# Turning x1 into tokens: TensorE transposes replaced by VectorE block transposes and on-chip DMAs

## The chip, the cores and the metric

The kernel runs on one core of a Trainium2 chip. The metric is device time in microseconds (us), the median of several runs. The page and the trace come from one further, profiled execution.

## The reference

Everything is float32, for 32 images of 128 channels x 64 x 64 pixels. The third line of the first block is a 3x3 convolution done in a learned "butterfly" transform domain.

```python
# layer 0
x = x + conv(group_norm(x))          # _gn, then _kop2d with the butterfly matrices
# layer 1, on tokens: t[b] is 4096 tokens x 128 channels
t = x.reshape(B, C, H * W).transpose(0, 2, 1)
t = t + attention(layer_norm(t))     # 128x128 probabilities per image, from the sum over tokens of k v^T
t = t + experts(layer_norm(t))       # 8 experts, the best 2 of each token, weighed by a softmax
x = t.transpose(0, 2, 1).reshape(B, C, H, W)
```

x1 below is x after layer 0, which lies with channels on partitions. Layer 1 needs it with tokens on partitions, 32 tiles of 128 tokens per image.

## The kernel before

The program has three stages in time. Stage one normalises each image, transforms it forward and puts it into DRAM (xf). Stage two multiplies in the transform domain, one of 64 columns after another, and puts the products into DRAM (pf). Stage three, which the change touches, takes the images one after another as a software pipeline: it loads r from pf, transforms back along w (`w_inverse`, copied into u by `w_out` on ScalarE), then along h (`h_inverse`), adds the image (`h_out`, on VectorE, which writes x1 into `ys[b]`), turns x1 into tokens, and runs attention and experts on them.

Every piece of work in stage three is an entry of a plan: a key, an engine, an estimated duration, what it comes after, and what room it takes (PSUM tiles "pe" and "tl", rings for r, and so on). The order in which pieces are issued is written out by hand in `ORDER`: a list of `key:stage` words for one period. Image b's piece stands at b + stage + (place in the list), shifted for the first two and the last two images by the numbers in `EDGE`. Each engine works strictly in that order, and so does SP, whose queue issues the DMAs. The keys used below:

- `r0` to `r7`, `x` (SP): loads of the transformed products and of the image.
- `w`, `wo`, `h`, `ho`: inverse along w, its copy by ScalarE, inverse along h, its sum by VectorE.
- `pt` (TensorE) and `to` (ScalarE), eight of each per image: `turn` transposes four 128x128 tiles of x1 into a PSUM tile (L1066), `turned` copies it into the token buffer `tk[b % 2]` (L1071). `pt` waits for `so` of the image two before, which last reads that buffer.
- `sa` (VectorE): the statistics of the tokens (L1035, L1037). `pwa`, `na` (ScalarE, GpSimd): their reciprocal root.
- `xg` (ScalarE, L1101) and `pg` (TensorE, L1112): the normalised tokens and their Gram matrix. `gs` to `prx`: the small chain of the attention's softmax.
- `pp`, `at`, `ad`: the attention's product, its scaling, its sum into the tokens (L1185, L1196, L1211), with the statistics for the second norm.
- `pwb` to `gt`: the router. `xn`, `px`, `xT`: normalised tokens, turned for the experts.
- `pe` (TensorE, L1323): the experts, two PSUM tiles of 128x512 per 128 tokens. `m` (VectorE, L1334) weighs them by the gates, `s` (GpSimd, L1359 to L1362) sums them into the tokens.
- `so` (VectorE, L1368): block transposes of the finished tokens. A VectorE transpose turns each block of 32x32 within its 32 partitions; the store `os` (SP, L1378) puts the blocks into their places in DRAM.
- `prep`: once, corrections of the weights for the norms' means.

The experts' PSUM tiles come from a pool of three (`eps`), the "tl" tiles from a pool of two.

Of the kernel before, what the change touches and what calls it, by code (L numbers as in the profile page):

```python
# [10 lines left out]
F32 = mybir.dt.float32  # L11
# [92 lines left out]
def kernel(  # L104
# [732 lines left out]
    kvb = kc.tile([P, 2, P], F32, name="kvb")  # L837
    nc.gpsimd.dma_start(kvb[:, 0, :], bk.partition_broadcast(P))
    nc.gpsimd.dma_start(kvb[:, 1, :], bv.partition_broadcast(P))
    u = up.tile([P, n, P], F32, name="u")  # L840
    tk = [ct.tile([P, NT, P], F32, name=f"tk{i}") for i in range(2)]
    xg = [ct.tile([P, 4, P], F32, name=f"xg{i}") for i in range(NG)]
# [26 lines left out]
    plan = Plan({"cv": 1, "pe": 3, "tl": 2, "r": 8, "xg": NG, "xn": 2, "tm": 2, "so": 2})  # L869
# [34 lines left out]
    def conv(b):  # L904
# [12 lines left out]
        def w_out(e, oh):  # L917
            def run():
                ps = tile_of["cv", b, e]
                for r in range(2):  # L920
                    nc.scalar.copy(  # L921
                        u[r * n : (r + 1) * n, :, oh * n + 8 * e : oh * n + 8 * e + 8],
                        ps[oh * n : (oh + 1) * n, :, r * n : (r + 1) * n].rearrange("h o w -> h w o"),
                    )
            return run
# [88 lines left out]
        for e in range(8):  # L1014
            at = b + 0.08 * e
            add(b, f"w{e}", "PE", 1.9, at, w_inverse(e), [f"r{e}"] + [(b - 1, f"h{k}") for k in range(4)], ("cv",), ("r",))
            for oh in range(2):
                add(
                    b, f"wo{e}_{oh}", "ACT", 1.2, at, w_out(e, oh),
                    [f"w{e}"] + [(b - 1, f"h{k}") for k in range(4)], (), ("cv",) if oh else (),  # L1020
                )
# [5 lines left out]
    def front(b):  # L1027

        t = tk[b % 2]
        v = {}  # L1030

        def bn(which, lo, hi):
            bs = st.tile([P, 4, 6], F32, name=f"bs{which}_{b}_{lo}", tag="bs", bufs=2)
            for i in range(lo, hi):
                nc.vector.bn_stats(bs[:, i - lo, :], t[:, i, :])  # L1035
# [24 lines left out]
        def turn(g):  # L1060
            def run():
                ps = tile_of["pt", b, g] = tps.tile([P, 512], F32, tag="tl", name=f"pt{b}_{g}")
# [6 lines left out]
        def turned(g):  # L1069
            def run():  # L1070
                nc.scalar.copy(  # L1071
                    t[:, 4 * g : 4 * g + 4, :].rearrange("p k c -> p (k c)"), tile_of.pop(("pt", b, g))
                )
            return run
# [10 lines left out]
        for g in range(8):  # L1085
            at = s1 + 0.016 * g
            add(b, f"pt{g}", "PE", 0.48, at, turn(g), [(b - 2, f"so{g}")] + [f"ho{k}" for k in range(4)], ("tl",))
            add(b, f"to{g}", "ACT", 0.55, at, turned(g), [f"pt{g}"], (), ("tl",))
            add(b, f"sa{g}", "DVE", 0.85, at, stats1(g), [f"to{g}"] + (["sa0"] if g else []))
        if b == 0:  # L1090
            add(b, "prep", "PE", 3.5, 1.2, prepare, [f"sa{g}" for g in range(8)], ("pe",), ("pe",))
        add(b, "pwa", "ACT", 3.1, s1 + 0.14, lambda: power(1), [f"sa{g}" for g in range(8)])
        add(b, "na", "POOL", 1.7, s1 + 0.14, lambda: newton(1), ["pwa"])


        def norm(g):
            def run():
                rstd, nmr, above = (v[1][:, k, :] for k in range(3))
                for k in range(4):
                    i = 4 * g + k  # L1100
                    nc.scalar.activation(  # L1101
                        xg[g % NG][:, k, :], t[:, i, :], AF.Identity, bias=above[:, i : i + 1], scale=rstd[:, i : i + 1]
# [3 lines left out]
        def gram(g):  # L1106
            def run():
                if g == 0:
                    v["pg"] = tps.tile([P, 512], F32, tag="tl", name=f"pg{b}")
                for k in range(4):  # L1110
                    i = 4 * g + k
                    nc.tensor.matmul(  # L1112
                        v["pg"][:, 0:P], xg[g % NG][:, k, :], xg[g % NG][:, k, :],
# [4 lines left out]
        for g in range(8):  # L1118
            at = s1 + 0.26 + 0.016 * g
            add(b, f"xg{g}", "ACT", 1.65, at, norm(g), ["na", (b if g >= NG else b - 1, f"pg{(g - NG) % 8}")], ("xg",))  # L1120
# [85 lines left out]
        def added(lo, m):  # L1206
            def run():
# [3 lines left out]
                nc.vector.tensor_tensor(t[:, lo : lo + m, :], ps[:, :, 0:P], t[:, lo : lo + m, :], ALU.add)  # L1211
# [79 lines left out]
    def experts(b):  # L1291
        t = tk[b % 2]

        def normal(g):
            def run():
                rstd, nmr = tile_of["norm", b]
                x = tile_of["xn", b, g] = wp.tile([P, 4, P], F32, tag="xn", name=f"xn{b}_{g}")
                for k in range(4):
                    i = 4 * g + k
                    nc.scalar.activation(  # L1300
                        x[:, k, :], t[:, i, :], AF.Identity, bias=nmr[:, i : i + 1], scale=rstd[:, i : i + 1]
# [39 lines left out]
        def weighed(i, half):  # L1341

            def run():
                ps = tile_of.pop(("pe", b, i, half))
                for e in range(4):
                    nc.vector.scalar_tensor_tensor(  # L1346
                        t[:, i, :], ps[:, e * P : (e + 1) * P], tile_of["gate", b][:, i, 4 * half + e : 4 * half + e + 1],
                        t[:, i, :], ALU.mult, ALU.add,
# [6 lines left out]
        def summed(j):  # L1355
            def run():
# [4 lines left out]
                for m in range(2):  # L1361
                    nc.gpsimd.tensor_tensor(t[:, lo : lo + 2, :], t[:, lo : lo + 2, :], tm[:, :, m, :], ALU.add)  # L1362
            return run

        def flip(g):
            def run():
# [3 lines left out]
                    in_=t[:, 4 * g : 4 * g + 4, :].rearrange("p t (k c) -> p t k c", c=32),  # L1370
# [44 lines left out]
    for b in range(B):  # L1415
# [5 lines left out]
        s1:4 px2:4 m4_0:4 pe5_0:4 xT2:4 m5_1:4 pwa:3 pe6_0:4 ho0:2 px3:4 pe4_1:4 h1:2 m4_1:4 xn6:4 m5_0:4 na:3  # L1421
        m6_0:4 pe6_1:4 ho1:2 s2:4 xg0:3 pe7_1:4 pe7_0:4 m7_0:4 m6_1:4 h2:2 xT3:4 so0:4 xg2:3 xg1:3 m7_1:4 pe8_0:4
        ho2:2 pe9_0:4 s3:4 m8_0:4 xg3:3 pe8_1:4 m9_0:4 pg0:3 m8_1:4 pg1:3 pe9_1:4 xg5:3 pe10_1:4 pe10_0:4 m9_1:4
        xg4:3 pe11_0:4 s4:4 m10_0:4 pg2:3 so1:4 pg3:3 xg6:3 os1:4 xg7:3 pg4:3 pe11_1:4 xn5:4 pg5:3 m11_1:4 m11_0:4
        pg6:3 r1:1 m10_1:4 pg7:3 s5:4 pe12_0:4 gs:3 pe13_1:4 m12_0:4 pb:3 pe12_1:4 t1:3 pe13_0:4 os0:4 r2:0 pb2:3
        h3:2 sm:3 m13_0:4 pr:3 xT4:4 sr:3 m12_1:4 sn:3 m13_1:4 pe14_0:4 s6:4 m14_0:4 pc:3 pe15_1:4 pe15_0:4 prx:3
        ho3:2 pp0:3 m15_0:4 px5:4 at0:3 pe14_1:4 m15_1:4 pe19_0:4 m14_1:4 xT5:4 ad0:3 pe18_0:4 xn7:4 s7:4 pp6:3
        m18_0:4 pe19_1:4 at6:3 pp9:3 w0:1 m19_0:4 m19_1:4 at9:3 ad6:3 pe18_1:4 r7:1 wo0_0:1 ad9:3 pe16_0:4 wo0_1:1
        pp21:3 m18_1:4 pe16_1:4 at21:3 m16_0:4 so3:4 s9:4 pp12:3 m16_1:4 w1:1 at12:3 ad21:3 r4:0 x:1 os3:4 pe17_1:4
        wo1_0:1 ad12:3 pe17_0:4 wo1_1:1 pp24:3 m17_1:4 pe22_0:4 m17_0:4 at24:3 s8:4 pp3:3 m22_0:4 w2:1 at3:3 ad24:3  # L1430
        pe23_0:4 ad3:3 wo2_0:1 pe22_1:4 wo2_1:1 pp30:3 m22_1:4 pe23_1:4 m23_0:4 at30:3 pp15:3 m23_1:4 w3:1 ad30:3
        at15:3 s11:4 so4:4 pe21_1:4 ad15:3 wo3_0:1 r5:0 os4:4 px6:4 pe20_0:4 wo3_1:1 pe20_1:4 m20_0:4 xT6:4 pp18:3
        m20_1:4 pe21_0:4 m21_1:4 at18:3 pp27:3 m21_0:4 w4:1 at27:3 s10:4 ad18:3 pe26_0:4 ad27:3 wo4_0:1 pe27_1:4
        pe26_1:4 m26_0:4 pwb:3 m27_1:4 pt0:2 so2:4 pe24_0:4 m26_1:4 pe27_0:4 m24_0:4 pt1:2 m27_0:4 to0:2 nb:3
        pe25_1:4 to1:2 so5:4 wo4_1:1 pe25_0:4 m25_1:4 os5:4 s13:4 px7:4 m25_0:4 pe24_1:4 xT7:4 l2:3 xn0:3 pt2:2 f1:3
        w5:1 f2:3 pt5:2 pe30_0:4 m24_1:4 wo5_0:1 f3:3 pe31_0:4 wo5_1:1 s12:4 pe30_1:4 m30_0:4 to2:2 to5:2 w6:1 sa0:2
        m31_0:4 m30_1:4 pe31_1:4 pt4:2 m31_1:4 pt3:2 to4:2 f4:3 pe28_1:4 px0:3 pe29_1:4 sa5:2 wo6_0:1 s15:4 sa4:2
        wo6_1:1 sa1:2 pe28_0:4 w7:1 xn1:3 f5:3 xT0:3 to3:2 m28_0:4 so6:4 m28_1:4 m29_1:4 os6:4 pe29_0:4 xn4:3 pt6:2
        m29_0:4 px1:3 gt:3 pe0_0:3 s14:4 to6:2 pe1_1:3 m0_0:3 r6:0 os2:4 pe0_1:3 m1_1:3 wo7_0:1 pe1_0:3 pe3_0:3
        px4:3 wo7_1:1 sa6:2 m1_0:3 m0_1:3 pe2_0:3 xn3:3 xn2:3 xT1:3 sa2:2 s0:3 pe3_1:3 m2_0:3 h0:1 m3_1:3 so7:4  # L1440
        m3_0:3 sa3:2 os7:4 pe2_1:3 pt7:2 r0:0 r3:0 pe4_0:3 pe5_1:3 m2_1:3 to7:2 sa7:2
# [3 lines left out]
            at:-0.001152 f:0.024239 gs:-0.002876 gt:0.000645 h:-0.088197 ho:-0.107173 l:-0.011950 m:-0.001978  # L1445
            na:-0.062269 nb:0.023962 os:0.037831 pb:-0.003357 pc:0.004368 pe:-0.004859 pg:-0.007392
            prep:-0.061921 prx:-0.000723 pt:-0.339605 pwa:-0.154931 pwb:0.037324 px:0.004889 r:-0.551854
            s:-0.000175 sa:-0.148905 sm:-0.006267 sn:0.000807 so:-0.001240 sr:0.003296 t:-0.002368 to:-0.321139
            w:-0.120521 wo:-0.109642 x:0.001867 xT:0.001275 xg:0.001692 xn:0.024691
        """,  # L1450
        1: """
            ad:0.003202 at:0.005763 f:0.005458 gs:-0.006322 gt:-0.000499 h:0.054990 ho:0.051746 l:-0.039944
            m:-0.001956 na:-0.011054 nb:-0.006237 os:0.010755 pc:-0.007414 pe:-0.000758 pg:0.001613 pr:-0.004399
            prx:-0.010090 pt:-0.015523 pwa:0.002034 pwb:0.001095 px:-0.002083 r:0.003449 s:-0.001956 sa:0.014227
            sn:-0.012403 so:-0.008148 sr:-0.010178 t:0.008140 to:0.002048 w:-0.000799 wo:-0.000193 xT:-0.009151
            xg:0.001343 xn:0.009969
        """,
        B - 2: """
            ad:-0.000137 at:0.005214 f:0.009800 gt:0.013838 h:-0.001798 ho:-0.002170 l:0.001614 m:0.011670
            na:0.002329 nb:-0.000549 os:0.199427 pb:-0.000148 pc:-0.004225 pe:0.008786 pg:-0.022172 pp:-0.005288  # L1460
            pr:-0.000058 prx:-0.004077 pt:-0.004342 pwa:-0.000635 pwb:-0.005281 px:0.016961 r:-0.007120
            s:0.049524 sa:-0.000213 sm:0.000159 sn:0.010880 so:0.176068 sr:0.012703 t:0.003951 w:0.001356
            wo:-0.009915 x:0.098978 xT:0.012789 xg:0.005833 xn:0.039799
        """,
        B - 1: """
            ad:0.016785 at:0.025250 f:0.011554 gt:0.005035 h:0.014633 ho:-0.003864 m:0.001746 na:0.022282
# [76 lines left out]
```

## Time and profile before

| | us |
|---|---|
| median of 3 runs (5923.06 to 5928.99) | 5924.06 |
| the profiled execution | 5924.1 |
| its span, first to last instruction | 5922.4 |
| stage three begins, about | 2542 |
| an image in the steady part of stage three | 101.8 |

On the page, busy time is the union of an engine's instructions; DMA-issuing instructions, which are all that SP runs, are not counted. "PE" is TensorE's matmuls, "PEld" its weight loads, "DVE" VectorE, "ACT" ScalarE, "POOL" GpSimd, "SPq" SP's queue. A row of the windows gives, for a stretch of time, its length, the busy time of each engine with its number of instructions, the granted TensorE clock, and the share and rate of DMA. A row of groups gives line, engine, operation, output and inputs, shape, count, then busy time and mean duration in ns, then the idle time ahead of it. A row of the timeline gives start, duration and what ran.

### The profile page before, as it was taken

The page shows a single profiled execution, that of the slowest core. Times are in us where ns is not written, and L with a number is a line of the kernel's source. Part 1 is how long each engine was busy: PE and PEld are TensorE (multiplying, and loading weights), DVE is VectorE, ACT ScalarE, POOL GpSimd, SP SyncE. Part 2 cuts the span into 40 slices and gives each one's busy share as a digit, 9 for nine tenths or more (in the row PEclk, how much of TensorE's full clock was granted, in tenths as well). Part 3 has the DMA queues.
Part 4 walks back from the last instruction along what each step waited for, and adds up shares of the span by engine and source line. Part 5 has one row for each costly group of instructions (what it writes and reads, how often), then busy time and mean ns, then how long its engine had stood idle before and what let it go on. Part 6 is the DMA issues. An engine that isn't in the chain of part 4 may idle for free. (4 is left out here: it accounts for less than half of the span.)

```text
span 5922.4 us, 221064 instructions
## 1 busy us (share of the span) xinstructions
PE 5789.1 (98%) x94348; PEld 4560.4 (77%) x94348; DVE 4235.4 (72%) x10353; ACT 3837.7 (65%) x7089; POOL 3947.6 (67%) x4210
## 2 busy tenths in 40 slices
PE   7999999999999999979999999999999999999997
PEld 7999999999999999976666666666666666666653
DVE  5565555555555555538888878788888888787877
ACT  7666664555555555557777777777777777777762
POOL 2110006666666666607888888888888888888887
PEclk9999999999999999989999999999999999999999
DMA  5767766666666666652323222233223222222201
GB/s 194 241 228 233 236 210 206 171 174 171 171 173 173 172 172 173 158 159 61 97 76 87 79 79 87 82 88 83 88 75 97 76 84 81 79 86 83 77 21 29
DMA packets 664681, 756.88 MB, mean 128 GB/s; under 512 B 70608, under 2 KB 462288, under 8 KB 659600
## 3 DMA queue, kind: packets, MB, share of 16 engines
q1 hardware_dynamic: 661088, 733.69, 43.0%
q8 instruction: 740, 12.12, 0.9%
q0 software_dynamic: 2608, 9.06, 0.5%
q14 instruction: 245, 2.01, 0.1%
HBM read 406.79 MB, written 335.54 MB: 125 GB/s over the span
## 5 line engine op out<-in xcount | busy, mean ns | idle before, releaser
L1323 PE MATMUL pe<-ew_sb,xT 128*128 128x512 f32 x4096 | 1973.2, 600 | 36.6 <-DVE tm L1334 22.8
L1334 DVE TENSOR_TENSOR tm<-pe,oh 128x512 f32<-128x512 f32 x2028 | 1298.4, 678 | 369.1 <-PE pe L1323 259.4
L1359 POOL TENSOR_TENSOR tm<-tm 128x512 f32<-128x512 f32 x1014 | 1270.4, 1272 | 287.0 <-DVE tm L1334 282.2
L1323 PEld LDWEIGHTS pe<-ew_sb,xT 128*128 128x128 f32 x4096 | 691.8, 190 | 552.1 <-issue 325.3
L660 DVE COPY f<-g 128x1024 f32<-128x1024 f32 x508 | 622.4, 1225 | 651.9 <-PE g L649 651.9
L671 PE MATMUL m<-f,s 128*64 128x64 f32 x32768 | 1071.3, 224 | 1.7 <-ACT f L660 0.8
L671 PEld LDWEIGHTS m<-f,s 128*64 128x64 f32 x32768 | 1001.1, 138 | 63.2 <-issue 2.5
L617 POOL COPY s<-l 128x512 f32<-128x512 f32 x512 | 546.2, 1102 | 527.3 <-issue 510.4
L660 ACT COPY f<-g 128x1024 f32<-128x1024 f32 x508 | 514.9, 1014 | 562.4 <-PE g L649 536.3
L1362 POOL TENSOR_TENSOR tk<-tk,tm 128x256 f32<-128x256 f32 x1014 | 737.9, 728 | 79.5
L1360 POOL TENSOR_TENSOR tm<-tm 128x512 f32<-128x512 f32 x507 | 644.7, 1272 | 39.8
L649 PE MATMUL g<-c,wst 9*128 9x128 f32 x16256 | 601.2, 284 | 4.5 <-issue 4.1
L921 ACT COPY u<-pu 64x512 f32<-64x512 f32 x960 | 558.0, 581 | 67.8 <-PE pu L910 58.7
L1196 ACT ACTIVATE pp<-pp,ln 128x128 f32<-128x128 f32 x1024 | 442.3, 432 | 230.9 <-PE pp L1185 157.2
L649 PEld LDWEIGHTS g<-c,wst 9*128 9x128 f32 x16256 | 504.0, 187 | 39.5 <-issue 4.8
L619 POOL TENSOR_SCALAR s<-l 128x512 f32<-128x512 f32 x256 | 509.6, 1991 | 0.0
L362 POOL TENSOR_TENSOR grstd<-gms,mhalf 128x1 f32<-128x1 f32 x32 | 17.7, 554 | 736.4 <-DVE gms L358 736.4
L431 PE MATMUL pf<-ph,v 128*128 128x128 f32 x4096 | 491.2, 278 | 5.5 <-ACT z L396 1.1
L910 PEld LDWEIGHTS pu<-qw,r 128*128 128x128 f32 x3840 | 456.8, 193 | 34.0 <-ACT u L921 22.2
L431 PEld LDWEIGHTS pf<-ph,v 128*128 128x128 f32 x4096 | 466.9, 192 | 15.5 <-ACT z L396 7.2
L910 PE MATMUL pu<-qw,r 128*128 128x128 f32 x3840 | 471.2, 276 | 4.9 <-ACT u L921 4.8
L1035 DVE BATCH_NORM_STATS2 bs<-tk 128x6 f32<-128x128 f32 x2048 | 449.5, 280 | 24.5 <-ACT tk L1071 23.2
(176 smaller groups left out, 7978.4 us busy)
## 6 DMA issues: line engine op xcount, KB each, us to landing
xf<-f SPq DMA_DIRECT2D x512, 256.0 KB
pf<-o SPq DMA_DIRECT2D x1016, 128.0 KB
l<-xf SPq DMA_DIRECT2D x1012, 128.0 KB
r<-pf SPq DMA_DIRECT2D x496, 256.0 KB
x<-in_x_dram SPq DMA_DIRECT2D x256, 256.0 KB
out_dram<-so SPq DMA_DIRECT2D x1024, 64.0 KB
y<-in_x_dram SPq DMA_DIRECT2D x31, 2048.0 KB
r<-pf POOLq DMA_DIRECT2D x16, 248.0 KB, 8.3
```

The source lines that it names most:

```text
L431: nc.tensor.matmul(pl[:, j * P : (j + 1) * P], vs[b][:, 8 * g + j, :], ph.rearrange("h r m -> h (r m)"), start=True, stop=True,)
L617: nc.gpsimd.tensor_copy(dst, src)
L649: nc.tensor.matmul(pg[g // 2][:, g % 2, m * P : (m + 1) * P], wst[rows, 16 * half + 4 * t + m, :], c[rows].rearrange("r h k -> r (h k)"), ...
L660: copy(f.rearrange("i m (g o) -> i m g o", g=2), tile_of["g", w, half, t][k].rearrange("i g (o m) -> i m g o", o=4))
L671: nc.tensor.matmul(ps[hh * n : (hh + 1) * n, q, :], s[:, h].rearrange("i k b -> i (k b)")[:, B * r : B * r + n], f[:, h, r, :], start=(r = ...
L910: nc.tensor.matmul(ps[:, k, :], rs[b, e][:, k * P : (k + 1) * P], qw.rearrange("w r m -> w (r m)"), start=True, stop=True,)
L921: nc.scalar.copy(u[r * n : (r + 1) * n, :, oh * n + 8 * e : oh * n + 8 * e + 8], ps[oh * n : (oh + 1) * n, :, r * n : (r + 1) * n].rearran ...
L1323: nc.tensor.matmul(ps, tile_of["xT", b, i // 4][:, i % 4, :], ew_sb[:, es, :].rearrange("d e c -> d (e c)"), start=True, stop=True,)
L1334: nc.vector.tensor_tensor(tile_of["tm", b, i // 2][:, i % 2, es, :], tile_of.pop(("pe", b, i, half)).rearrange("p (e c) -> p e c", c=P), t ...
L1359: nc.gpsimd.tensor_tensor(tm[:, k, 0:4, :], tm[:, k, 0:4, :], tm[:, k, 4:8, :], ALU.add)
L1360: nc.gpsimd.tensor_tensor(tm[:, :, 0:2, :], tm[:, :, 0:2, :], tm[:, :, 2:4, :], ALU.add)
L1362: nc.gpsimd.tensor_tensor(t[:, lo : lo + 2, :], t[:, lo : lo + 2, :], tm[:, :, m, :], ALU.add)
```

## The change

Images 0 and 1 keep the transposes by TensorE, now in "pe" PSUM tiles. For the other 30, `turn` becomes a VectorE block transpose of 128x512 elements of x1 (`tr`, eight per image) into a small tile `tt`, two groups of four tiles side by side. After every second one `moved` (`td`, four per image) issues 16 DMAs on SP, each of 32 partitions x 1 KB, that bring the blocks into the token buffer. That buffer is now laid out as (partition, k, tile, 32) and read through a view, so that a token's 128 channels are four runs of 32. `td` waits for its two `tr` and for the flips `so` of the image two before; `sa` waits for `td`.

Beside it: for images 0 and 1 every second `xg` runs on VectorE. The second copy of each `w` of image 2 runs on VectorE. The four tiles `xg` are used in turn over all images, two of them lie in `ebb`'s memory, and the last holds `kvb` until `prep` has run. `prep` no longer waits for the statistics. ORDER and EDGE are new throughout: the convolution of an image is earlier by some 0.6 of a period, the moves `td` stand between the other SP work, and image 0's and 1's transposes and statistics are drawn together.

```diff
-    kvb = kc.tile([P, 2, P], F32, name="kvb")
...
-    tk = [ct.tile([P, NT, P], F32, name=f"tk{i}") for i in range(2)]
-    xg = [ct.tile([P, 4, P], F32, name=f"xg{i}") for i in range(NG)]
+    tk = [ct.tile([P, 4, NT, 32], F32, name=f"tk{i}") for i in range(2)]
+    tokens = [t.rearrange("p k i c -> p i k c") for t in tk]
+    xg = [ebb[:, 0:4, :], ebb[:, 4:8, :]] + [ct.tile([P, 4, P], F32, name=f"xg{i}") for i in range(2, NG)]
+    kvb = xg[NG - 1][:, 0:2, :]
...
         def turn(g):
             def run():
-                ps = tile_of["pt", b, g] = tps.tile([P, 512], F32, tag="tl", name=f"pt{b}_{g}")
+                if g % 2 == 0:
+                    tile_of["tt", b, g // 2] = wp.tile([P, 4, 8, 32], F32, tag="tt", name=f"tt{b}_{g}")
+                x1 = ys[b].rearrange("c l v a w -> c (l v) a w")
+                nc.vector.transpose(
+                    out=tile_of["tt", b, g // 2][:, :, 4 * (g % 2) : 4 * (g % 2) + 4, :].rearrange("p a i c -> p i a c"),
+                    in_=x1[:, 4 * g : 4 * g + 4],
+                )
+            return run
+
+        def turn_on_pe(g):
+            def run():
+                ps = tile_of["pt", b, g] = eps.tile([P, 512], F32, tag="pe", name=f"pt{b}_{g}")
...
+        def moved(c):
+            def run():
+                tt = tile_of.pop(("tt", b, c))
+                for k in range(4):
+                    for a in range(4):
+                        nc.sync.dma_start(
+                            tk[b % 2][32 * a : 32 * a + 32, k, 8 * c : 8 * c + 8, :].rearrange("p i c -> p (i c)"),
+                            tt[32 * k : 32 * k + 32, a].rearrange("p i c -> p (i c)"),
+                        )
+            return run
...
-            add(b, f"pt{g}", "PE", 0.48, at, turn(g), [(b - 2, f"so{g}")] + [f"ho{k}" for k in range(4)], ("tl",))
...
+            add(b, f"tr{g}", "DVE", 0.7, at, turn(g), [f"ho{k}" for k in range(4)] + ([f"tr{g - 1}"] if g % 2 else []), ("tt",) if g % 2 == 0 else ())
+            if g % 2:
+                add(b, f"td{g // 2}", "SP", 6.4, at, moved(g // 2), [f"tr{g - 1}", f"tr{g}", (b - 2, f"so{g - 1}"), (b - 2, f"so{g}")], (), ("tt",), 3.0)
...
-            add(b, "prep", "PE", 3.5, 1.2, prepare, [f"sa{g}" for g in range(8)], ("pe",), ("pe",))
+            add(b, "prep", "PE", 3.5, 1.2, prepare, (), ("pe",), ("pe",))
```

## The prediction

> **What bounds the kernel now.** I read the page's share of busy time and its forty slices first, then the busy time of each engine by stage.
>
> ```profile
> PE 5789.1 (98%) x94348; PEld 4560.4 (77%) x94348; DVE 4235.4 (72%) x10353; ACT 3837.7 (65%) x7089; POOL 3947.6 (67%) x4210
> ```
>
> ```profile
> core 0: us, PE busy (x) PEld busy (x) DVE busy (x) ACT busy (x) POOL busy (x), PEclk, DMA share, GB/s
> 4319.30:4421.10 101.80, 101.61 (x712) 68.26 (x711) 85.73 (x273) 75.58 (x168) 87.15 (x96) 1.00 0.29 84
> ...
> 2542.00:2690.00 148.00, 117.03 (x1992) 102.76 (x1987) 65.66 (x283) 90.23 (x191) 13.15 (x38) 0.90 0.50 139
> 2690.00:5680.00 2990.00, 2983.88 (x20942) 2003.34 (x20941) 2510.66 (x7932) 2211.79 (x4922) 2559.96 (x2792) 1.00 0.28 82
> 5680.00:5922.40 242.40, 194.33 (x626) 92.29 (x624) 193.08 (x567) 96.83 (x232) 194.91 (x205) 0.97 0.09 24
> ```
>
> The change lies wholly in the third stage, from 2542 us on. The reader sees three parts there. From 2690 to 5680 us TensorE is busy 99.8% at full clock: one image every 101.8 us, with VectorE at 85.7, GpSimd at 87.2 and ScalarE at 75.6 us of that. Ahead of it 148 us fill the pipeline, behind it 242 us drain it, and in both TensorE has gaps. In the middle only TensorE's own work counts.
>
> **What goes from TensorE.** Per image 32 transposes. A row's duration includes the depth of the pipeline, so I take starts: from a group's start to the next work's start.
>
> ```profile
> 4395.97 0.60 PE L1066 MATMUL pt<-ident,x 128*128 128x128 f32 x4
> 4396.41 1.95 PE L910 MATMUL pu<-qw,r 128*128 128x128 f32 x16
> ...
> 4403.85 1.04 PE L1066 MATMUL pt<-ident,x 128*128 128x128 f32 x8
> 4404.73 1.02 PE L1323 MATMUL pe<-ew_sb,xT 128*128 128x512 f32 x2
> ```
>
> ```profile
> 2690.00:5678.00 2988.00, 134.69 (x928) 113.18 (x928) 1.00 0.28 82
> ```
>
> Four take 0.44 us and eight take 0.88 us, so 32 take 3.5 us. The second fence is the transposes' line alone, over the saturated part: 928 of them, which is 29 images. So 29 x 3.5 = 101.5 us can go. Images 0 and 1 keep theirs; the records of image 31's fall into the drain, where TensorE has gaps, and count nothing.
>
> Here the Trainium skill speaks against the change: "VectorE: DVE Perf Modes", section "Rules for kernel authors", sends a 128x128 transpose to TensorE where PSUM will do, and its table of three paths prices one at 390 ns there (bf16). By that price 32 would take 12.5 us and 29 images 362 us. The rows above show 0.11 us each when queued back to back; I take the rows. The rule counts the cheapest transpose, but the engine it names is the full one.
>
> **What comes to VectorE.** Eight block transposes per image. The nearest row is the output's transpose, same shape and size:
>
> ```profile
> L1368 DVE STREAM_TRANSPOSE so<-tk 128x512 f32<-128x512 f32 x78 | 54.9, 704 | 0.6 <-DMA r<-pf 0.4
> ```
>
> ```profile
> 4391.15 0.70 DVE L1368 STREAM_TRANSPOSE so<-tk 128x512 f32<-128x512 f32 x1
> 4391.78 1.85 DVE L1334 TENSOR_TENSOR tm<-pe,oh 128x512 f32<-128x512 f32 x3
> ```
>
> From start to start 0.63 us, so 8 x 0.63 = 5.0 us: 85.7 + 5.0 = 90.7 us of a period of 101.8 - 3.5 = 98.3. VectorE's slack falls from 16.1 to 7.6 us. Can TensorE stay full beside so dense a VectorE? Before shows it for a while:
>
> ```profile
> 4366.00:4376.00 10.00, 10.00 (x61) 7.62 (x60) 9.79 (x39) 9.00 (x23) 9.24 (x9) 1.00 0.58 185
> ```
>
> I cut the new ORDER list into 16 equal parts and summed each part's TensorE and VectorE work from these rows' start-to-start times. Parts 2 and 3 leave VectorE some 6 us short of work; in the other 14 the two sums are within 2 us of each other. PSUM lets TensorE lead by three expert tiles (3 x 0.86 us), so most differences are absorbed, not all. I take 0.5 us of new stall per image, 29 x 0.5 = 15 us; the ends are 0 (all absorbed) and 3.5 us (the slack is too lumpy, everything eaten).
>
> **Views with runs of 32.** Statistics, norms, sums and flips now read tokens as 4 x 32. No row shows just this. Near rows: VectorE's sum of x1 (L942) runs over inner 16s and takes 1216 ns for 1024 elements, a flat copy (L660) 1225; ScalarE's scattered copy (L921) 581 ns, the flat one (L1316) 586, both 512 elements; GpSimd's regrouping copy (L617) 1102 ns for 512 against 1272 for the flat sum (L1359). So nothing. The other end: GpSimd's slack is 98.3 - 87.2 = 11 us, so each of its 32 sums into tokens could grow by 0.35 us before it became the bound. ScalarE loses eight copies of 0.58 us, not on the path.
>
> **The transfers.** Each image adds 64 DMAs of 32 KB on SP. The rows of the output stores:
>
> ```profile
> L1378 SPq DMA_DIRECT2D out_dram<-so x1024: 315/434/1850, 2711.5 to 5919.3; - x171
> ...
> 5390.59 8.71 DMA out_dram<-so
> ```
>
> One issue takes 434 ns, some 0.45 us with its gap; the first landing of such a store comes a median 1.76 us after its issue by the semaphore updates, but 8.71 us in the chain of waits when an image load is under way. SP issues about 24 us per image now (33 x 0.45 + 16 x 0.55); 64 x 0.45 = 29 us more makes 53 of 98. The extra 2 MB on today's 8.4 MB at 29% DMA share make about 36%. "DMA: Bandwidth & Descriptors" (Trainium skill, sections on the anatomy of one DMA and on measured bandwidth) again warns: about 2 us fixed each, and under 64 KB the descriptors dominate. Taken one after another that is 64 x 2 = 128 us, longer than the period, and 29 x 26 = 750 us slower. The trace has eight semaphores in turn, so eight fly at once, and stores follow each other at 0.45 us; I count the issue.
>
> The move waits for its transposes and for the flips of the image two before, which empty the token buffer. Behind it on SP stand the loads of r, of x and the stores; VectorE's statistics wait for its landing, and behind these in VectorE's queue stand the products that free TensorE's PSUM. The last move of an image (td3) stands right behind so7. Summing TensorE's durations along ORDER, so7 is at 78 us and the last statistics at 92 us of the period. td3 needs 16 x 0.45 + 1.76 = 9 us: 5 us of cover. td0, td1 and td2 have 73, 46 and 15 us to their statistics. td1 follows a burst of r loads (5.35 us to land in the chain), which its 46 us absorb. The new semaphore waits on VectorE are taken early, beside the instruction that runs, as at L1368 now: nothing. If all moves landed late, all would come back through that queue.
>
> **The head.** prep moves from behind image 0's statistics to the front of TensorE's queue. It needs wkv and prx, which land at 2554.0 and 2555.1 us; the first conv of image 0 ran from 2542.6 to 2562.8 us with 16.5 us of work. It now starts near 2556: +10 us. Against that: prep's 4.6 us (2603.0 to 2607.6) and the wait before it go; half the norms of images 0 and 1 move from ScalarE (6.3 us per four groups, 2603.6 to 2609.9) to VectorE, idle there for 12 us; and the statistics of image 0 no longer wait between groups. More conv work is in front of the first expert (101 us of TensorE work by my sum, 90 before), so less is left. I take -5 us, between -15 and +10. Moving half of image 2's w copies to VectorE (16 of about 0.6 us) falls where VectorE has gaps: nothing; uncovered, 10 us, outside the likely case.
>
> **The drain.** Convs run 0.6 slot earlier, so after image 31's last conv matmul stand 207 us of TensorE work instead of 179, and 231 instead of 197 of VectorE's, which has the longer queue. The drain grows by 34 us, of which 28 is work taken from the middle: +6 us, between -5 and +15.
>
> **Sum.** -101.5 + 15 - 5 + 6 = -85.5 us. The profiled execution took 5924.1 us around a span of 5922.4, the median run 5924.06, so both give the same: **5838 us**. Its own range: -101.5 - 15 gives 5808; +40 of stall, +5 head, +10 drain gives 5878.
>
> **Rivals.**
> 1. VectorE becomes the co-bound. For: 90.7 of 98.3 us, with waits it can't fill (in ten images 81.9 us on experts, 16.5 us on the softmax's matmul). Against: the waits on experts are there because TensorE is the slower engine. If it keeps 10 us idle, the period is 100.7 and 29 x 1.1 = 32 us are saved: 5892; with 8 to 11 us idle, 5834 to 5920.
> 2. Slower: td3's landing takes the place of the transposes. If it meets slow landings, its 16 transfers go in two rounds of eight at 8.7 us, 18 us after so7 with issue, 4 to 5 us later than the last statistics' place; VectorE stops with the expert products behind it, and TensorE after three tiles. At 4.7 us per image less the 3.5 saved: 29 x 1.2 = +35 us, 5959. It decides from 17.5 us after so7. For: SP is in order and stores can hold its lanes. Against: the image load x stands behind td3 in ORDER, the r burst far ahead.
> 3. The change doesn't do what it says: the views of 32 lengthen every row by as much as the transposes cost, and the time stays near 5924.
>
> **Chances.** The forecast 0.64, rival 1 0.16, rival 2 0.16, rival 3 0.04. About 0.2% (12 us) is what a measurement here can tell from no change. Faster 0.78 (forecast and nearly all of rival 1), same 0.04, slower 0.18 (rival 2 and the bad end of 1). The range, 5806 to 5920, takes in rival 1 and leaves out rival 2 and the forecast's low tail, about 0.2.
>
> **What would show it.** Right: the period in the middle near 98.8 us with TensorE above 99%; VectorE near 92%; block transposes of x1 at about 0.70 us; statistics not waiting on DMA; GpSimd's sums into tokens still 728 ns. Wrong: the first statistics idle on landings (rival 2); VectorE over 95% or TensorE waiting on its products (rival 1); longer rows at the token views (rival 3); a head longer than 158 us or a drain longer than 290.

## The result, and the profile after

The change made the kernel slower: 5954.9 us median of 4 runs (5950.7 to 5963.7) against 5923.6 us (5920.1 to 5929.0) for the kernel before on the same chip, ratio 1.0054 (95% interval 1.0037 to 1.0071). The forecast was 5838. The profiled execution took 5963.7 us around a span of 5961.8, and is the slowest of the four; the parts below are set against the 5922.4 us span of before.

The page's first row of the changed kernel, then its windows: one period, head, middle.

```profile
PE 5731.5 (96%) x93388; PEld 4472.5 (75%) x93388; DVE 4408.8 (74%) x10641; ACT 3659.8 (61%) x6801; POOL 3940.7 (66%) x4210
```

```profile
core 0: us, PE busy (x) PEld busy (x) DVE busy (x) ACT busy (x) POOL busy (x), PEclk, DMA share, GB/s
4302.60:4403.90 101.30, 98.99 (x680) 64.69 (x680) 90.69 (x280) 70.30 (x161) 86.93 (x96) 1.00 0.37 105
2547.70:2733.70 186.00, 127.55 (x2150) 118.18 (x2149) 77.51 (x308) 73.89 (x152) 7.74 (x31) 0.82 0.40 114
2733.70:5680.00 2946.30, 2872.89 (x19620) 1874.90 (x19619) 2631.24 (x8072) 2032.05 (x4620) 2518.40 (x2752) 1.00 0.37 103
```

Three things are to be seen. TensorE is no longer full in the middle (97.5%, before 99.8%). VectorE does 90.7 us per period, as forecast. And the head is longer, 186 us, with a mean granted clock of 0.82 (before 0.90); the prediction had named a head above 158 us as a sign that it was wrong.

To compare runs I use three points of the trace: the end of stage two's last matmul (L671), the start of the first expert matmul of image 0 ("first expert"), and the step from one image's first expert to the next image's (median of the 24 steps from the fifth on). "Head" is the time from the first point to the second. Stages one and two have the same code in every kernel here, and yet they end anywhere from 2542.8 to 2555.9 us in the traces of this case, so a first expert counted from the span's start would take in their scatter.

| | stages one and two | head | first expert | step | sum of 31 steps | last image's first expert to the end |
|---|---|---|---|---|---|---|
| before | 2542.8 | 136.6 | 2679.4 | 101.83 | 3151.6 | 91.4 |
| after | 2547.7 | 186.0 | 2733.7 | 101.35 | 3143.0 | 85.1 |
| difference | +4.9 | +49.4 | +54.3 | -0.48 | -8.6 | -6.3 |

4.9 + 49.4 - 8.6 - 6.3 = +39.4 us, the difference of the spans. The 4.9 us are not the change's. So there are two questions: what makes the head 49 us longer, and why a step that lost 3.5 us of TensorE's work is only 0.5 us shorter.

What came to VectorE and SP in one period, and GpSimd's sums into tokens on the page:

```profile
L1094 SPq DMA_DIRECT2D tk<-tt x65: 507/589/1102, 4302.5 to 4403.9; - x65
L1067 DVE STREAM_TRANSPOSE tt<-x x8: 669/685/703, 4310.6 to 4393.8; 128x512 f32<-128x512 f32 x8
```

```profile
L1405 POOL TENSOR_TENSOR tk<-tk,tm 128x256 f32<-128x256 f32 x1014 | 737.0, 727 | 79.5
```

The transposes take 0.69 us and the token views cost GpSimd nothing (727 ns, before 728). A move's issue takes 0.59 us, more than the 0.45 I had counted. The 2 us and the 64 KB that the prediction takes from "DMA: Bandwidth & Descriptors" stand, in the sections it names, for DMAs issued from GpSimd; no run here times one of these moves alone.

### The profile page after: what moved, and what is told of

The parts are those of the page before. It is cut to its first block, busy times and chain, and to the rows that moved or that the text cites. A ratio compares the mean times of both kernels' runs of the same rounds, so it can differ in the third digit from the quotient of the medians.

```text
span 5961.8 us, 222481 instructions
## 1 busy us (share of the span) xinstructions
PE 5731.5 (96%) x93388; PEld 4472.5 (75%) x93388; DVE 4408.8 (74%) x10641; ACT 3659.8 (61%) x6801; POOL 3940.7 (66%) x4210
## 4 chain that ended last, share of the span: by engine, by line
PE 70%; DVE 19%; ACT 3%; issue 3%; POOL 2%; DMA 1%; SPq 1%; DVEq 0%; POOLq 0%; ACTq 0%
PE pe L1365 19%; PE m L671 17%; PE g L649 9%; PE pf L431 7%; DVE tm L1376 5%; PE pu L911 4%; PE pg L1152 3%; PE py L935 3%; PE pv L409 3%; DVE sc L1255 3%; DVE bs L1037 3%; DVE tk L1251 2%; PE pz L386 1%; ACT z L396 1%; DVE so L1411 1%
## 5 line engine op out<-in xcount | busy, mean ns | idle before, releaser
L671 PE MATMUL m<-f,s 128*64 128x64 f32 x32768 | 1075.9, 224 | 3.1 <-issue 2.3
L671 PEld LDWEIGHTS m<-f,s 128*64 128x64 f32 x32768 | 1005.7, 139 | 64.7 <-issue 4.0
L1402 POOL TENSOR_TENSOR tm<-tm 128x512 f32<-128x512 f32 x507 | 643.9, 1270 | 39.8
L1342 ACT ACTIVATE xn<-tk,ln 128x128 f32<-128x128 f32 x1024 | 418.2, 484 | 131.4 <-POOL ln L1056 130.6
```

The source lines that it names most:

```text
L671: nc.tensor.matmul(ps[hh * n : (hh + 1) * n, q, :], s[:, h].rearrange("i k b -> i (k b)")[:, B * r : B * r + n], f[:, h, r, :], start=(r = ...
L1402: nc.gpsimd.tensor_tensor(tm[:, :, 0:2, :], tm[:, :, 0:2, :], tm[:, :, 2:4, :], ALU.add)
```

## Experiments on the head

What TensorE did there in the changed kernel (timeline: start, duration, what, idle time ahead of it and its releaser), and the clock:

```profile
2547.67 1.98 PE L850 MATMUL pm<-ew_sb,om 128*128 128x512 f32 x4
2559.54 1.19 PE L858 MATMUL pmk<-wkv,om 128*128 128x256 f32 x2 [9.89 <-DMA wkv<-in_wvT_dram]
2560.53 0.43 PE L866 MATMUL pms<-prx,om 128*128 128x8 f32 x2
2560.89 1.98 PE L963 MATMUL pw<-qw,r 128*64 128x64 f32 x32
2563.60 1.98 PE L963 MATMUL pw<-qw,r 128*64 128x64 f32 x32 [0.73 <-ACT u L972]
2566.26 1.98 PE L963 MATMUL pw<-qw,r 128*64 128x64 f32 x32 [0.69 <-ACT u L972]
```

```profile
2560.00:2590.00 30.00, 23.11 (x370) 20.98 (x371) 0.99 (x4) 6.30 (x11) 0.00 (x0) 0.50 0.43 112
```

prep stands first and waits for wkv. Then the pieces of image 0's convolution wait, one after another until 2587.5 us, 0.69 us for ScalarE's copy of the piece before, which I read as one PSUM buffer used in turn, and at half the granted clock they take 1.98 us each. TensorE is busy 77% of these 30 us.

**prep later.** Only its place in the order is changed.

```diff
-prep:-3.119807
+prep:-1.090800
```

> The changed kernel with the preparation (prep) moved from the front of TensorE's queue to the place between image 0's and image 1's convolutions; all else stays. Theory A (prep at the front costs the head: 9.9 us of idle waiting for wkv, then sixteen conv pieces at half the granted clock, one after another through one PSUM buffer): image 0's pieces run from about 2548 to 2568 us as in the kernel before, the first expert comes at 2706 to 2712 us instead of 2733.7, and the time falls by 22 to 27 us to about 5930. Rival B (something later in the head, image 2's convolution or the chain of attention, sets the first expert): the pieces end earlier, the first expert still comes within 5 us of 2733.7, time 5950 to 5955.

First expert 2709.3, as expected; the head is 163.6 us, 22.4 shorter; step unchanged (101.33); time 5938.9 us, ratio to before 1.0019 (1.0010 to 1.0027). By the medians that is 16 us less, short of the expected 22 to 27 (the profiled runs differ by 26, but the changed kernel's was its slowest). Theory A holds for the head, and 27 of its 49 us stay.

**prep first, in other PSUM buffers.** This splits the 22 us into waiting and what follows it.

```diff
-pe = eps.tile([P, 512], F32, tag="pe", name=...)     # pm0, pm1, pmk, pms
+pe = tps.tile([P, 512], F32, tag="tl", name=...)
```

> The changed kernel with prep still at the front, but its four PSUM tiles taken from the pool of the attention's tiles (tag tl), so that image 0's conv pieces find three free buffers. The wait for wkv stays. If the serial use of one buffer is what keeps TensorE's density at 73% and so the clock at half: pieces follow each other without the 0.69 us waits, the clock is back at 1.00 within about 10 us, image 0's last piece ends near 2581 us instead of 2594.8, time 10 to 14 us lower (about 5942). If the clock stays at half whatever the density: 16 pieces of 1.98 us end near 2592.6, time 2 to 3 us lower.

```profile
2556.76 1.19 PE L858 MATMUL pmk<-wkv,om 128*128 128x256 f32 x2 [8.39 <-DMA wkv<-in_wvT_dram]
2557.74 0.43 PE L866 MATMUL pms<-prx,om 128*128 128x8 f32 x2
2558.10 9.41 PE L963 MATMUL pw<-qw,r 128*64 128x64 f32 x268
```

The wait for wkv is still there, but more than eight pieces (32 matmuls each) now run in one row without a gap, and the clock in 2560 to 2570 us is 0.94. First expert 2714.4, the head 169.5 us: 16.5 of the 22.4 us were the one buffer with its half clock, 5.9 the wait and prep's place. Time 5946.5 us, ratio 1.0029 (1.0017 to 1.0040), 8 us less where 10 to 14 were expected.

**The kernel before, with prep first.**

```diff
-add(b, "prep", "PE", 3.5, 1.2, prepare, [f"sa{g}" for g in range(8)], ("pe",), ("pe",))
+add(b, "prep", "PE", 3.5, 1.2, prepare, (), ("pe",), ("pe",))
-prep:-0.061921
+prep:-3.361921
```

> The kernel before with one thing changed: prep at the front of TensorE's queue, as in the changed kernel. Theory A: TensorE waits for wkv until about 2554 to 2560 us, image 0's pieces then run at half clock and one by one until about 2590 us; less the 4.6 us that prep no longer takes at 2603 us, the first expert comes 20 to 27 us later (2700 to 2706 us) and the time is 5944 to 5951. My prediction's sum (+10 for the wait, less 4.6 and the wait ahead of it) would give 5924 to 5930.

```profile
2557.12 1.19 PE L857 MATMUL pmk<-wkv,om 128*128 128x256 f32 x2 [9.72 <-DMA wkv<-in_wvT_dram]
2558.11 0.43 PE L865 MATMUL pms<-prx,om 128*128 128x8 f32 x2
2558.47 9.63 PE L961 MATMUL pw<-qw,r 128*64 128x64 f32 x267
```

A miss for theory A as I had put it: the same wait, but the pieces run on, and the head is 146.8 us, 10.2 longer, not 20 to 27. Time 5936.1 us, ratio 1.0014 (1.0006 to 1.0023), which misses the 5924 to 5930 of my prediction's sum as well. Being first costs the wait; the 16.5 us come only where the pieces also get one buffer in turn. Which buffer a tile gets is settled when the program is built; why the two programs differ there was not followed.

**Image 2's copies back on ScalarE** (with prep late), against the other 27 us.

```diff
-copy = nc.vector.tensor_copy if b == 2 and oh else nc.scalar.copy
+copy = nc.scalar.copy
```

> The changed kernel with prep late, and image 2's second copies from PSUM back on ScalarE as in the kernel before. If these copies on VectorE (0.70 us each, 16 of them, with the next conv step waiting for the one PSUM buffer) lengthen the head: first expert 5 to 12 us before 2709. If VectorE's gaps hide them, as my sum had it: within 3 us of 2709, time within 6 us of the run with late prep alone. If ScalarE is the fuller engine there: 5 us or more later.

First expert 2710.0, head 163.1 us, time 5938.4 us: no effect, as the prediction had it.

## Experiments on the step

TensorE's only wait over ten steps of the changed kernel, in the view of waits (us in all, times, longest), and the chain of waits at one of the two places where it leaves TensorE:

```profile
PE pe L1365 <- DVE tm L1376: 20.8, 20, 2.1
```

```profile
4412.77 1.73 PE pe L1365 x4
...
4414.53 0.69 DVE tm L1376
4415.22 0.46 DVE tk L1251
4415.68 0.15 DVE sc L1255
...
4439.58 0.60 DVE tm L1376
...
4440.22 1.13 PE pe L1365 x2
```

From 4414.5 to 4440.2 us the chain stays on VectorE: eight of an image's eleven attention sums (tk, router sums sc, statistics) with expert products (tm) between them. A second stretch of 9.1 us, at 4461.5, is the gates. None of the new transposes is in the chain of this period: two stand just ahead of the long stretch (4411.9 us), the next behind it (4449.2 us). That left two theories: **C**, VectorE's total density, and **D**, the new order of the work, whatever the transposes do.

**Copies by ScalarE in place of the transposes.**

```diff
-nc.vector.transpose(out=tt..., in_=x1[:, 4 * g : 4 * g + 4])
+nc.scalar.copy(tt..., x1[:, 4 * g : 4 * g + 4])
```

> The changed kernel with the eight block transposes of each image from 2 on replaced by ScalarE copies with the same operands and places (the tokens are then not turned, so the output is another one); transfers, waits and order stay. Theory C (the 5 us of transposes on VectorE make it so dense that its stretches stand in TensorE's way): VectorE falls to 85.6 us per period and the step between images falls from 101.35 to 98.3 to 99.0 us, the time by 68 to 88 us to 5865 to 5886. Rival D (the new order itself, with its long stretch of attention sums on VectorE, stalls TensorE whatever the transposes do): step 100.8 or more, the time falls by less than 20 us.

Step 102.43, longer by 1.1; time 5991.3 us, ratio 1.0104 (1.0088 to 1.0119). Against C, but not clean, as ScalarE has new work in its queue.

**Four elements copied in place of each transpose.**

```diff
-nc.vector.transpose(out=tt..., in_=x1[:, 4 * g : 4 * g + 4])
+nc.vector.tensor_copy(tt[..., 0:4], x1[:, 4 * g : 4 * g + 1, 0, 0:4])
```

> The changed kernel with the block transposes left out: in each one's place VectorE copies four elements a partition (the tokens moved on chip are then not those of the image), with the same waits, places and transfers. This takes 4.5 us per period off VectorE and puts nothing elsewhere, which the ScalarE copies of the run before did not (they held ScalarE 0.6 us each). Theory D: only the two groups ahead of the dense half and the two inside it count, step falls by 1.0 to 2.2 us to 99.2 to 100.4. Theory C: all 4.5 us count, step 98.3 to 98.8. If the order alone stalls TensorE: step stays above 101.

Step 101.44, time 5967.2 us: against C, and against D as put here. But a copy took 0.46 us on average and VectorE fell by only some 1.5 us per period, so this said little by itself.

**No transposes at all.**

```diff
-nc.vector.transpose(out=tt..., in_=x1[:, 4 * g : 4 * g + 4])
```

> The changed kernel with nothing at all in the places of VectorE's block transposes (the transfers move zeros, so tokens are not those of the image; order and transfers stay). The run with the four-element copies still spent 3.5 us a period on VectorE on them; here VectorE has 5.4 us less than in the changed kernel and no other engine has more. Theory D (the order; the chain of waits passes through no transpose): step within 0.5 us of 101.35, time 5935 to 5955. Theory C (VectorE's total density): step 98.3 to 99.3, time 5866 to 5896.

Ten steps each, first the changed kernel, then this run:

```profile
3731.10:4744.60 1013.50, 989.97 (x6751) 646.80 (x6748) 904.85 (x2791) 702.66 (x1597) 867.73 (x949) 1.00 0.38 105
```

```profile
3749.80:4763.30 1013.50, 990.29 (x6792) 647.21 (x6791) 864.13 (x2720) 703.74 (x1601) 869.98 (x951) 1.00 0.37 105
```

VectorE has 4.1 us less per period, and the step is 101.35 again; time 5958.2 us, ratio 1.0050 (1.0037 to 1.0062). C is out, and the chain still passes the same two stretches. What VectorE saved it waited (first the changed kernel, then this run, where L1375 is the same line):

```profile
DVE tm L1376 <- POOL tk L1405: 37.4, 28, 2.2
DVE tm L1376 <- PE pe L1365: 36.8, 51, 1.4
```

```profile
DVE tm L1375 <- POOL tk L1404: 62.2, 39, 3.0
DVE tm L1375 <- PE pe L1364: 45.9, 80, 1.8
DVE x L947 <- PE py L938: 10.6, 19, 0.9
```

**Router sums merged**, which shortens VectorE inside the attention's stretch.

```diff
-for k in range(m):
-    nc.vector.scalar_tensor_tensor(
-        sc[:, 0, lo + k, :], ps[:, k, P : P + NE], v[1][:, 0, lo + k : lo + k + 1], v["lq", lo][:, k],
-        ALU.mult, ALU.add)
+part = sc[:, 0, lo : lo + m, :]
+nc.vector.tensor_tensor(part, ps[:, :, P : P + NE],
+    v[1][:, 0, lo : lo + m].unsqueeze(2).to_broadcast([P, m, NE]), ALU.mult)
+nc.vector.tensor_tensor(part, part, v["lq", lo][:, 0:m], ALU.add)
```

> The changed kernel with the 32 small router sums of an image (one of about 0.25 us for each block of 128 tokens, in the attention's sums) done for three blocks at once by a multiply and an add: 22 instructions in place of 32, some 2.5 us less on VectorE, all of it in its dense half. Theory D: TensorE gets all of that back until its own work bounds it, step 98.3 to 99.5 us, time 54 to 88 us lower. Theory C (density alone, 2.5 of 10.7 us of idle more): also lower, but by less than half of it, step 100.2 or more. If neither, and the period hangs on the queue of GpSimd or on transfers: step unchanged.

```profile
3733.60:4730.70 997.10, 979.69 (x6792) 648.85 (x6791) 881.04 (x2701) 703.31 (x1601) 869.92 (x951) 1.00 0.37 107
```

```profile
PE pe L1365 <- DVE tm L1376: 17.4, 10, 1.7
```

Step 99.72, just above D's range; time 5903.1 us, ratio 0.9959 (0.9947 to 0.9972). VectorE has 2.4 us less per period, not even as much as in the run without transposes, and 1.63 us of it reach the step, about the share (8 of 11) that lies in the chain's stretch: the place counts, not the amount. TensorE's waits were 20 in ten steps and are 10 now, once a period for 1.7 us at the gates; the attention's stretch has left the chain.

**The same in the kernel before**, as a control.

> Control: the kernel before the change with the router sums merged. There TensorE is busy 99.8% of the steady stretch and VectorE waits for it, so 2.5 us less on VectorE should bring nothing: step 101.8, time within 8 us of the kernel before. If it gains 20 us or more, VectorE bound that kernel too and the reading of its profile was wrong.

Step 101.35, time 5903.0 us, ratio 0.9956 (0.9943 to 0.9970). A miss: 24.7 us gained by the medians where I expected 8 at most; in the profiled runs 14 us of it lie in the steps and 8 in the last two. The kernel before, on ten steps (first row, before; second, this run):

```profile
3698.00:4716.00 1018.00, 1016.14 (x7109) 682.31 (x7108) 857.50 (x2721) 755.36 (x1681) 871.53 (x950) 1.00 0.29 84
```

```profile
3699.30:4712.80 1013.50, 1012.12 (x7113) 683.15 (x7112) 837.08 (x2621) 754.48 (x1682) 871.92 (x951) 1.00 0.29 84
```

99.8% busy did not mean that TensorE's work alone set the step, as the prediction had taken it to: its busy time shrank by 0.4 us per period with the same matmuls. So TensorE's own work is at most 101.35 us with the 32 transposes and 101.35 - 3.5 = 97.9 without. The changed kernel loses at least 3.5 us per step, of which 2.4 show as idle time. And with merged sums in both the two kernels take the same time, 5903.1 and 5903.0 us.

**Two transposes moved** behind the gates.

```diff
-pp0:3 tr6:2 ... tr7:2 at0:3 ... h1:1 tr4:2 ... so5:4 tr5:2 ... m0_0:3 so7:4 wo1_0:0 pe0_1:3
+pp0:3 tr4:2 ... tr5:2 at0:3 ... h1:1 ... so5:4 ... m0_0:3 tr6:2 so7:4 wo1_0:0 tr7:2 pe0_1:3
```

> The changed kernel with two of the eight block transposes of an image moved in the order of the work: groups 4 and 5 take the places of 6 and 7, and 6 and 7 now stand after the gates, where the chain of waits runs through TensorE and VectorE has gaps. VectorE does just as much as before per period. Theory D (VectorE's dense half, from the attention's sums to the gates, is what holds the period; 1.26 us of it go to the other half): the step between images falls from 101.35 by 0.6 to 1.3 us, the time by 17 to 37 us. Theory C (the total density of VectorE counts): step within 0.2 us of 101.35, time within 6 us.

```profile
PE pe L1365 <- DVE tm L1376: 28.6, 30, 2.1
```

Step 102.45, time 5994.4 us, ratio 1.0109 (1.0095 to 1.0123): neither theory's number. The places I had read as gaps, just behind the gates, are where TensorE waits for the first products; TensorE has ten waits more in ten steps, 8 us in all. Again the place decides.

**Two flips moved** out of and behind the gates.

```diff
-f4:3 so6:4 f5:3 ... m0_0:3 so7:4 wo1_0:0 pe0_1:3 m1_0:3 td3:2 px2:3 wo1_1:0 m1_1:3 pe2_0:3
+f4:3 f5:3 ... m0_0:3 wo1_0:0 pe0_1:3 m1_0:3 px2:3 wo1_1:0 m1_1:3 so6:4 pe2_0:3 ... so7:4 ... td3:2
```

> The changed kernel with the last two flips of an image's output (so6 inside the gates, so7 between the first products behind them) moved behind the first four products that follow the gates, and the move td3 with them. VectorE's work stays the same. If the stretch through the gates holds the period: 1.3 us leave the chain, step 100.0 to 100.8 us, time 16 to 40 us lower. If only the attention's sums hold it: step within 0.3 us of 101.35, time within 9 us. If td3 now lands too late for the statistics: step above 101.6.

Step 101.31, time 5956.4 us: nothing. The chain of this run shows why:

```profile
4461.84 0.20 DVE tops L1307
...
4462.06 0.24 ACT tops L1311
...
4462.58 0.35 DVE tops L1316
```

With so6 gone VectorE waits here for ScalarE's exponential; the flip had only filled that wait.

**Gates earlier**, between the last products of the image before.

```diff
-l2:3 xn1:3 pe29_1:4 ho3:1 ... m29_0:4 w0:0 xT0:3 f1:3 ... f2:3 ... f3:3 ... f4:3 ... f5:3 w1:0 ... gt:3 m0_0:3
+l2:3 xn1:3 pe29_1:4 f1:3 ho3:1 ... f2:3 f3:3 ... f4:3 f5:3 m29_0:4 w0:0 xT0:3 ... gt:3 ... w1:0 ... m0_0:3
```

> The changed kernel with the gates of an image (f1 to gt) moved forward in the order: they stand between the last expert products of the image before, as in the kernel before the change, instead of behind them all. No work changes. If the new order is what holds the period and the gates are one of its two places (TensorE idles 1.7 of its 2.3 us per period there): step 99.6 to 100.7 us instead of 101.35, time 19 to 50 us lower. If the period hangs on the attention's sums alone: step within 0.3 us of 101.35, time within 9 us.

```profile
ACT tops L1311 <- DVE tops L1307: 57.9, 10, 5.8
```

```profile
PE pe L1365 <- ACT xT L1358: 26.7, 10, 2.7
PE pe L1365 <- DVE tm L1376: 3.0, 10, 0.3
```

Steps of 103.6 and 104.5 in turn (median 104.03), time 6050.0 us, ratio 1.0203 (1.0189 to 1.0217). TensorE's wait for the products is gone, but ScalarE now stands 5.8 us a period at the exponential with xT queued behind it, and TensorE waits for xT. I then put the exponential behind xT (`xT0:3 f5:3`):

> The changed kernel with the gates earlier as in the run before, but their exponential (f5) left behind xT on ScalarE. If only that exponential spoiled the earlier run: step 100.0 to 101.3 us, below the changed kernel's 101.35, time 5920 to 5954. If the gates between the products slow the release of TensorE's PSUM buffers whatever ScalarE does: step above 101.6, time above 5960.

```profile
PE pu L911 <- ACT u L923: 19.1, 10, 1.9
```

Steps of 103.0 and 104.7 mixed, time 6029.9 us, ratio 1.0177 (1.0163 to 1.0191): now u's copies stand behind the exponential, and TensorE waits for those. So the 1.7 us at the gates stay unexplained in one respect: what order would free them.

## Edits together

> The changed kernel with prep between the convolutions of images 0 and 1 and the router sums merged. If the head's 24 us and the merged sums' 1.6 us a step are separate causes they add: first expert near 2709 us, step 99.7 us, time 5878 to 5886. If the period's relief depends on the phase that the head sets: step above 100.2, time 5895 or more.

prep late and sums merged: head 160.5 us, step 99.70, time 5883.0 us, **ratio 0.9925 (0.9912 to 0.9937)**: the two causes add up, and this version beats both kernels. More than half of that gain is not the change's, since merged sums alone bring the kernel before to 5903.0: with sums merged in both and prep late, the change is worth 20 us.

> The same with the two flips moved as well. If the two stretches on VectorE hold the period one after the other: step 98.2 to 99.2 us, time 5840 to 5868. If merging has already freed the chain of both: step 99.7, time 5878 to 5886.

With the flips moved too: step 99.68, 5882.8 us. The other three sums, each with prep late and merged sums, carried the failed edits' cost with them: with two transposes moved 5914.8 us (step 100.77), with the gates earlier 5984.7 (102.71), with the exponential behind xT 5964.1.

> Three edits of these runs together in the changed kernel: prep between the convolutions of images 0 and 1, two transposes moved behind the gates, router sums merged. If the head and VectorE's dense half are the two places where the change lost its gain: first expert near 2709 us, step 98.3 to 99.0 us, time 5936 less 29 x 2.3 to 3.0, so 5848 to 5870, some 55 to 75 us faster than the kernel before. If the period hangs on something else: 5920 to 5940.

> Three edits together in the changed kernel: prep between the convolutions of images 0 and 1, router sums merged, gates earlier. If these are the places where the gain was lost: first expert near 2709 us, step 98.3 to 99.2 us (TensorE's own work is 98.1), time 5840 to 5868. If merging and moving the gates relieve the same stall: step 99.7 as with merging alone, time 5878 to 5884.

> Late prep and merged sums (5883 us, step 99.7) with the gates earlier and the exponential behind xT. If the gates' stretch is what is left (TensorE waits 1.7 us there once a period): step 98.2 to 99.3 us, time 5840 to 5872. If moving the gates costs VectorE's queue more than it gives: step above 99.9, time above 5890.

## Why the prediction was wrong, step by step

- **"In the middle only TensorE's own work counts"**: not so. The control gained 0.48 us per step in the kernel before by shortening VectorE's sums alone.
- **TensorE's 3.5 us per image**: right in the main. With merged sums in both kernels its busy time per step is 101.2 us before and 98.0 after.
- **VectorE's 5.0 us per image**: right in size (85.7 + 5.0 = 90.7 forecast, 90.7 measured), and without effect: the step is the same with no transposes at all.
- **"I take 0.5 us of new stall per image"**: this term failed. The step was forecast at 98.8 and is 101.35, so 2.55 us more of stall in each of 29 steps, 74 us. Its upper end, 3.5 us ("the slack is too lumpy, everything eaten"), is near what happened. The forecast compared the sums of work in 16 parts of ORDER and let three PSUM tiles absorb the rest; it did not follow which VectorE rows TensorE's PSUM tiles wait for. Shown by runs: the attention's sums are such rows, and 1.63 us of the stall goes when they are shortened. The gates still hold 1.7 us by the view of waits; three edits there failed, so that cause is read from the trace and not shown. Cumulative sums along the order do not settle it either: from `pp0` to `ad30` they give 37.5 us on TensorE against 39.8 on VectorE now (25.9 and 24.9 before), but the 39.8 hold three transposes, 1.9 us, and without them the step did not move.
- **The head, -5 us**: this term failed too, +49.4 measured. prep's own move cost 10.2 us in the kernel before, where my terms (10 of wait, less prep's 4.6 and a wait) gave 5.4 at most. What I did not see is that the conv pieces would share one PSUM buffer and that the half clock of the idle stretch would then stay: 16.5 us. Together 22.4. Of the other 27 us some 12 are TensorE's work: with prep late it is busy 118.0 us in the head, 105.6 before, and the whole inverse along h of image 2 stands ahead of the first expert, where before none of it did. The prediction had counted this (101 us for 90) and entered it as a gain. The last 15 us were not settled; copies on VectorE are not part of them.
- **The drain, +6 us**: the forecast's sums were right. From the last conv matmul to the end it was to grow by 34 us, to 231 of VectorE's work; it grew by 33.0 (first row, before; second, after):

```profile
5676.40:5922.40 246.00, 197.93 (x640) 94.30 (x638) 195.88 (x572) 97.23 (x233) 198.43 (x208) 0.97 0.09 24
5682.80:5961.80 279.00, 230.29 (x738) 111.44 (x738) 231.37 (x683) 116.49 (x284) 231.49 (x247) 0.95 0.13 35
```

  What of it is paid back in the steps, as the forecast assumed for 28 us, can't be told from the runs. The table cuts elsewhere: from the last image's first expert on it is 6.3 us shorter.
- **The forecast's sum**: 74 (stall) + 4 (the first steps and one step of 103.4) + 54 (head, 49.4 against -5) + 5 (stages one and two) - 12 (the table's last column, -6.3 against +6) = 125 us, from 5838 to 5964, the profiled execution.
- **Rivals.** Rival 1 named VectorE as co-bound by its density, at a step of 100.7, with TensorE waiting on its products as the sign. The sign is there and the step is near, but the density is not the cause: VectorE paces the step in certain rows, whatever the transposes do. Rival 2 put the time at 5959, close to the 5955 measured; that is chance, as no landing of a move shows among VectorE's waits. Rival 3: rows at the token views keep their length.

The rule of the clock bears on the head. The Trainium skill, "TensorE: Matmul & The Clock Gate", section "Part 1: The HAM clock gate", says that about 3.4 us of sustained activity bring the clock back. With pieces back to back it did: in the run with other PSUM buffers the window from 2560 us, two microseconds after the first piece, is at 0.94. In the changed kernel, with a 0.69 us wait after each piece, it stayed at 0.50, until six pieces ran without a gap from 2587.5 us on (windows of the changed kernel):

```profile
2587.50:2591.20 3.70, 3.66 (x68) 3.66 (x70) 0.00 (x0) 0.59 (x1) 0.00 (x0) 0.50 0.50 142
2591.20:2595.00 3.80, 3.80 (x132) 3.79 (x128) 0.00 (x0) 2.34 (x4) 0.00 (x0) 0.99 0.43 109
```

3.7 us of gapless work brought the full clock, which agrees with the page. The share of busy time alone does not decide: in the run with other buffers TensorE was busy 78% of 2570 to 2580 us, with one wait of 2.2 us, and the mean clock was 0.83. By the rule alone the wait for wkv would have cost its 10 us and, an estimate from that page, some 2 us of slow clock (half of 3.4 us); by the runs prep's place cost 22.

## What to carry to other kernels

Work taken from the full engine is worth only what the order lets through: see which rows of the other engines the chain of waits passes. Sums of work by part of the order, which the forecast used, did not find them here. Taking load off an engine outside that chain gives nothing (4 us of VectorE, no change), 2.4 us inside it gave 1.6. A 99.8% busy engine may still be paced by another one. And an edit that helps the changed kernel belongs into the kernel before as well: more than half of what the best version gains comes without the change. Before moving one-time work to the front of a queue, ask what it waits for and which buffers it leaves to the work behind it.

## What the runs showed of the hardware

- Short waits can hold the half clock: 0.50 all through 2560 to 2590 us, with 0.69 us of waiting in every 2.67 until 2587.5, and the full clock 3.7 us after the waits ended.
- Among these small VectorE operations three times the elements took no longer: the router sum of one block (8 elements a partition) takes 233 ns, a multiply and an add for three blocks (24) take 181 and 191. Each row gives the operation's minimum, median and maximum in ns:

```profile
L1255 DVE SCALAR_TENSOR_TENSOR sc<-pp,ln,lq x317: 211/233/236, 3732.7 to 4742.6; 128x8 f32<-128x8 f32 x159
```

```profile
L1255 DVE TENSOR_TENSOR sc<-pp,ln x110: 172/181/183, 3787.0 to 4716.9; 128x24 f32<-128x24 f32 x100, 128x16 f32<-128x16 f32 x10
L1258 DVE TENSOR_TENSOR sc<-sc,lq x110: 182/191/192, 3787.2 to 4717.1; 128x24 f32<-128x24 f32 x100, 128x16 f32<-128x16 f32 x10
```

- TensorE's busy time, as the profile counts it, is elastic: with the same matmuls it fell from 101.6 to 101.2 us per period when VectorE's sums got shorter.
